# Late expert blocks as two halves of 64 rows, each with an expert of its own, multiplied in two halves of TensorE's columns

## The chip, the core and the metric

One core of one Trainium2 chip runs the whole program in one launch. The metric is the device time of that launch in microseconds (us). TensorE multiplies: its array of 128 x 128 holds a stationary operand (up to 128 columns, loaded by an LDWEIGHTS that the profile shows as PEld) and streams a moving operand through it; the result lands in PSUM, one partition for each stationary column. VectorE (DVE), ScalarE (ACT) and GpSimd (POOL) do the elementwise work, SyncE (SP) issues most DMAs, GpSimd the indirect ones. All data are float32.

## The reference

Two layers on x of 4 batches x 512 tokens x 512 channels. Layer 0 is a gate (a two-sided decayed sum over the 512 positions), a Mamba2 state-space block, a second gate and a feed-forward part with experts. Layer 1 is a gate, an attention block (16 heads in 4 groups), a gate and a dense feed-forward part. The change lies in layer 0's experts, which compute this, with E = 8 experts and the two best of them for each token:

```python
logits = x @ gate_w.T + gate_b
top_vals, top_idx = jax.lax.top_k(logits, 2)
routing = softmax(top_vals)
for e in range(8):
    h = x @ w1[e].T + b1[e]                  # w1[e]: 1024 x 512
    x_glu, x_lin = h[:, 0::2], h[:, 1::2]
    y = x_glu * sigmoid(1.702 * x_glu) * (x_lin + 1.0)
    ye = y @ w2[e].T + b2[e]                 # w2[e]: 512 x 512
    out = out + ye * sum(routing * (top_idx == e))[:, None]
```

Here x is 2048 tokens x 512 channels, the output of the second gate. The reference multiplies every token by every expert. Only 2 x 2048 = 4096 pairs of a token and an expert have a weight that is not zero.

## The kernel before, in words

**Blocks.** The kernel computes only those 4096 pairs. It sorts them by expert into blocks of 128 rows, and a block has one expert. How many blocks an expert needs is known only when the routing has been computed on the chip, so the program holds NBLK = 39 blocks, as many as any routing can need, of which ALWAYS = 37 are always run and the last two stand behind a branch on the number of blocks in use (L1557).

**Early and late.** The batches come out of the Mamba2 stage one after the other. Full blocks of the first three batches can be formed before the fourth is routed: at least NEARLY = 17 of them, the *early* blocks, which the program interleaves with the end of the Mamba2 stage of the fourth batch (`rounds()`, L1297). The other 22 are *late* blocks and run after it. The late blocks are again ordered so that those with rows of batch 0 come first (FIRST = 15 of them), because the layer's next step starts with batch 0.

**Finding the rows.** `route()` (up to L620) computes for each pair its block and its place in it. It builds tables with VectorE (`ov`, `os`) and multiplies them on TensorE (`ptok`, L604), two times four matmuls with VectorE's second pair of tables between them, so that `toks` holds in column s and row v the id of the pair in place s of block v. `logits()` (L498) is in front of it: for each quarter of the batch the products `pl`, and transposes `pht` of the gated rows, which go to a table `rows_h` in HBM. `order_blocks(lo, hi)` (L648) then decides which blocks of the table become the program's blocks lo to hi-1. It is called for the early blocks (L1437) and for the late ones (L1537). VectorE finds which blocks are in use; TensorE sums them (`pidx<-use`, L663 and following); VectorE builds a selection `of` (L686); TensorE multiplies with it (`pidx<-of`, L689 and L690); VectorE turns the result into `idx_h` (which rows to fetch), `eb` (the expert of each block) and `idx_o` (where to scatter). All blocks that follow wait for this.

**A round.** `class Experts` runs the blocks as a pipeline, one `round()` (L865) for each block i. Every product is 4 matmuls of a 128 x 128 stationary piece with 512 moving columns:

- `fetch` (L771): GpSimd gathers the 128 rows of block i+3 from `rows_h` by an indirect DMA.
- `flip` (L783): TensorE transposes the rows of block i+1 (`pfl`, 4 transposes), ScalarE copies them into `hT`.
- `first_half`: `pg` (L812), then `pn` (L823), the two halves of w1 for block i, with biases, Tanh and products on VectorE and ScalarE between.
- `finish` (`pyt`): 4 transposes of block i-1's y; ScalarE copies them, halved, into `yT`.
- `down` (`po`, L845): the product with w2 for block i-2, a bias on VectorE, and GpSimd's scatter into `rows_o` (L851).

A block of the table that is not in use writes its rows to row 0 of `rows_o`, which nobody reads.

**Weights.** An expert's weights are two halves of w1 (`w<-in_w1x`, 1 MB each), w2 (1 MB) and broadcast biases b1 and b2 (512 and 256 KB). SyncE reads the expert of a block from `eb` and issues the loads under the condition that it differs from the one that the slot holds. Early blocks use slot 0. Late blocks use slot i % 2, so that a late block's weights are loaded while the block before it runs. `second_weights` (L857) loads w2 when the last `down` that reads the slot has been issued.

**What sets the order.** The program is written as one stream, and a scheduler orders the instructions of each engine from it by a priority that is, roughly, the place in the stream, and by when it expects the operands to be ready: an instruction that waits can be overtaken by a later one that is ready, when the program is built. On the chip each engine then runs its instructions in that fixed order. `with after(engine)` (L88) pins the instructions in it behind the one of that engine that was recorded last. `more()` (L1523) runs late rounds, and after each it lets `pump` issue pieces of layer 1's gates (VectorE's `num`, `den`, `eu` with ScalarE), 1 or 2 per round. During the last rounds, `load_results` (L1481) and `add_results` bring batch 0's rows back from `rows_o` and transpose them on TensorE (`pcb`, L1500) into x.

L1190 (`pyd`) and L1033 (`ppr`), which the prediction's steps use as rows, belong to the Mamba2 stage: L1033 has a stationary operand of 64 columns between matmuls of 128.

Of the kernel before, what the change touches and what calls it, by code (L numbers as in the profile page):

```python
# [36 lines left out]
NBLK = (B * T * TOPK + E * (P - 1)) // P  # L37
NROW = B * T * TOPK + 1

NEARLY = -(-((B - 1) * T * TOPK - E * (P - 1)) // P)  # L40

ALWAYS = NBLK - 2

FIRST = (T * TOPK + E * (P - 1)) // P
# [39 lines left out]
def block_kernel(ctx: ExitStack, tc: tile.TileContext, a: dict, out: bass.AP):  # L84
# [374 lines left out]
    res_id = [count(f"res{c}", [[TOPK * T, B], [P, NT]], 1, 1 + c * T) for c in range(2)]  # L459
# [6 lines left out]

    places = tmp.tile([P, NBLK], I32, tag="th", name="places")
    for lo, hi in ((0, FIRST), (FIRST, ALWAYS - NEARLY), (ALWAYS - NEARLY, NBLK - NEARLY)):
        half = (hi - lo + 1) // 2
        nc.gpsimd.iota(places[:, lo : lo + 2 * half], pattern=[[1, half], [half, 2]], base=lo,  # L470
                       channel_multiplier=0)
    place = rt.tile([P, NBLK - NEARLY], F32, name="place")
    nc.vector.tensor_copy(place, places[:, : NBLK - NEARLY])
# [171 lines left out]
    eb = rt.tile([1, NBLK + 1], I32, name="eb")  # L645
    in_use = eb[:, NBLK:]

    def order_blocks(lo, hi):  # L648

        n = hi - lo  # L650
        cv = rt.tile([P, 1], F32, tag="cv", name="cv")
        nc.vector.tensor_tensor(jk, sel, cnt[:, (N2 if lo else N2 - NT), :], ALU.mult)
        nc.vector.tensor_reduce(cv, jk, AX.X, ALU.add)
        use = rt.tile([P, 1], F32, tag="use", name="use")
        if lo == 0:
            nc.vector.scalar_tensor_tensor(use, v_lo, float(P), cv, ALU.add, ALU.is_le)
        else:
            nc.vector.tensor_tensor(use, v_lo, cv, ALU.is_lt)
            nc.vector.tensor_tensor(use, use, taken, ALU.subtract)
        pi = ps_tp("pidx")  # L660
        rank = rt.tile([P, 1], F32, tag="vrank", name="vrank")
        if lo == 0:
            nc.tensor.matmul(pi[:, P : P + 1], lhsT=tri_lt, rhs=use, start=True, stop=True)  # L663
            nc.vector.tensor_copy(rank, pi[:, P : P + 1])
        else:

            two = rt.tile([P, 2], F32, tag="two", name="two")
            nc.vector.tensor_tensor(jk, sel, cnt[:, NT, :], ALU.mult)
            nc.vector.tensor_reduce(rank, jk, AX.X, ALU.add)
            nc.vector.tensor_scalar(two[:, 0:1], v_lo, rank, use, ALU.is_lt, ALU.mult)  # L670
            nc.vector.tensor_tensor(two[:, 1:2], use, two[:, 0:1], ALU.subtract)
            nc.tensor.matmul(pi[:, P : P + 2], lhsT=tri_lt, rhs=two, start=True, stop=True)
            nc.tensor.matmul(pi[:, P + 2 : P + 3], lhsT=ones, rhs=two[:, 0:1], start=True, stop=True)
            nc.tensor.matmul(pi[0:1, P + 3 : P + 4], lhsT=ones[:, 0:1], rhs=use, start=True, stop=True)
            nc.vector.tensor_copy(in_use, pi[0:1, P + 3 : P + 4])

            nc.vector.tensor_scalar(
                rank, pi[:, P + 1 : P + 2], pi[:, P + 2 : P + 3], two[:, 1:2], ALU.add, ALU.mult
            )
            nc.vector.scalar_tensor_tensor(  # L680
                rank, pi[:, P : P + 1], two[:, 0:1], rank, ALU.mult, ALU.add
            )
        if lo == 0:
            nc.vector.scalar_tensor_tensor(taken, rank, float(n), use, ALU.is_lt, ALU.mult)
        of = tmp.tile([P, NBLK], F32, tag="th", name="of")
        nc.vector.tensor_scalar(  # L686
            of[:, :n], place if lo else lane[:, :n], rank, use, ALU.is_equal, ALU.mult
        )
        nc.tensor.matmul(pi[:, :n], lhsT=toks, rhs=of[:, :n], start=True, stop=True)  # L689
        nc.tensor.matmul(pi[0:1, 2 * P : 2 * P + n], lhsT=v_e, rhs=of[:, :n], start=True, stop=True)  # L690

        gf = tmp.tile([P, NBLK], F32, tag="th", name="gf")
        nc.vector.tensor_scalar(gf[:, :n], pi[:, :n], NROW - 2.0, None, ALU.add)
        nc.vector.tensor_copy(idx_h[:, lo:hi], gf[:, :n])
        low = tmp.tile([P, NBLK], I32, tag="th", name="low")
        nc.vector.tensor_scalar(
            low[:, :n], idx_h[:, lo:hi], T - 1, (B - 1) * T, ALU.bitwise_and, ALU.bitwise_xor
        )
        nc.vector.tensor_scalar(
            idx_h[:, lo:hi], idx_h[:, lo:hi], 1, (B - 1) * T,  # L700
            ALU.logical_shift_right, ALU.bitwise_and,
        )
        nc.vector.tensor_tensor(idx_h[:, lo:hi], idx_h[:, lo:hi], low[:, :n], ALU.bitwise_xor)
        ef = tmp.tile([1, NBLK], F32, tag="th", name="ef")
        nc.vector.tensor_scalar(ef[:, :n], pi[0:1, 2 * P : 2 * P + n], E - 1.0, None, ALU.add)
        nc.vector.tensor_copy(eb[:, lo:hi], ef[:, :n])
        nc.vector.tensor_copy(idx_o[:, lo:hi], pi[:, :n])

    class Experts:
# [13 lines left out]
        def open(self):  # L723
# [5 lines left out]
            self.load_w1(1, 0, 0)  # L729
            self.load_w2(0, 0)  # L730
# [9 lines left out]
        def slot(self, i):  # L740
            return 0 if i < NEARLY else i % 2

        def load_w1(self, h, s, e, **kw):

            nc.sync.dma_start(
                out=self.w1[s][h].rearrange("p k i -> p (k i)"),
                in_=a["w1x"][e, :, h * NC * I : (h + 1) * NC * I], **kw
            )
            if h == 1:
                nc.sync.dma_start(  # L750
                    out=self.b1[s].rearrange("p a i -> p (a i)"),
                    in_=a["b1x"][e].partition_broadcast(P), **kw
                )

        def load_w2(self, s, e, **kw):
            nc.sync.dma_start(out=self.w2[s].rearrange("p k m -> p (k m)"), in_=a["w2x"][e], **kw)
            nc.sync.dma_start(out=self.b2[s], in_=a["b2x"][e].partition_broadcast(P), **kw)

        def know(self, n):
# [4 lines left out]
            if n > NEARLY:  # L764
                self.weights(self.i if n == NBLK else NEARLY)
# [22 lines left out]
        def weights(self, i, early=False):  # L788
# [3 lines left out]
            s = self.slot(i)  # L792
            e = nc.sync.value_load(eb[0:1, i : i + 1], min_val=0, max_val=E - 1)
            kw = {"cond": e != self.held[s]} if s in self.held else {}
            self.held[s] = e
            self.reg[i] = s, bass.ds(e, 1), kw
            self.load_w1(0, *self.reg[i][:2], **kw)
# [4 lines left out]
        def more_weights(self, i):  # L802
            if i in self.reg:
                s, e, kw = self.reg[i]
                self.load_w1(1, s, e, **kw)

        def first_half(self, i):

            s, hT, sm = self.reg[i][0], self.hT.pop(i), self.sm
            pg = ps_mm("pg")  # L810
            for k in range(NC):
                nc.tensor.matmul(  # L812
                    pg, lhsT=hT[:, k, :], rhs=self.w1[s][0][:, k, :],
# [1208 lines left out]
```

## Time and profile before

| what | value |
|---|---|
| median of 3 runs | 2245.44 us (2244.33 to 2245.93) |
| the profiled execution's own time | 2248.54 us |
| its span (first to last instruction) | 2246.8 us |
| mean granted TensorE clock | 0.978 of full speed |
| TensorE busy by stage, us of the stretch | 0 to 664: 589.79 of 664.00 |
| | 664 to 790: 119.65 of 126.00 |
| | 790 to 890: 96.05 of 100.00 |
| | 890 to 1123: 231.62 of 233.00 |
| | 1123 to 2246.8: 1094.71 of 1123.80 |
| VectorE busy, 890 to 1123 | 146.44 |
| DMA engines busy, 890 to 1123 | 0.82 (296 GB/s) |

How to read it. The span is counted from the first recorded instruction; the time of the execution is 1.7 us longer because it has what lies around the instructions. The early blocks start within the stretch 664 to 790, when the fourth batch is still in the Mamba2 stage and being routed, and the late blocks fill the stretch 890 to 1123. A line of the trace such as `L812 MATMUL pg<-w,hT 128*128 128x512 f32 x8` tells the kernel's line, the tile written and the tiles read, the stationary operand (rows * columns), the moving one, and how many records follow each other; a float32 matmul leaves two records. In a timeline the first two columns are the start and how long the group took, and what stands in brackets is the time for which the engine was idle before it, and who released it.

### The profile page before, as it was taken

The numbers are of one execution on the slowest core, as the hardware profiler recorded it, in microseconds if no ns is written. First come the engines' busy times: TensorE is split into PE (matmuls) and PEld (weight loads), VectorE is DVE, ScalarE is ACT, GpSimd is POOL, SyncE is SP. The second block draws the span as 40 slices with busy tenths as digits, with TensorE's granted clock in tenths as the row PEclk, the third lists the DMA queues.
The fourth block names the chain that finished last, engine by engine and source line by source line (L and its number), as shares of the span: only waits on it lengthen the run. The fifth ranks groups of instructions, "written<-read, shape, count | busy, mean of one in ns | idle before, by whom it ended". The sixth has DMA issues, their size and how long they took to land. (4 is left out here: it accounts for less than half of the span.)

```text
span 2246.8 us, 23747 instructions
## 1 busy us (share of the span) xinstructions
PE 2131.8 (95%) x7528; PEld 1228.1 (55%) x7528; DVE 1526.6 (68%) x3039; ACT 969.5 (43%) x1899; POOL 451.5 (20%) x620
## 2 busy tenths in 40 slices
PE   2879999999999999999988999999999999999998
PEld 1445565565665444444444455555555555568887
DVE  8698989989753556666477766677767765555332
ACT  4476676765842233433154333333334332333221
POOL 4023232331222111222112111112212122100000
PEclk9889999999999999999989999999999999999999
DMA  7542252341433357988576655555645564531100
GB/s 257 176 146 71 95 164 74 128 141 67 135 124 126 146 201 268 367 299 310 206 241 200 188 183 150 159 164 176 183 143 173 142 195 141 178 130 38 38 20 20
DMA packets 112452, 357.38 MB, mean 159 GB/s; under 512 B 14592, under 2 KB 23168, under 8 KB 102912
## 3 DMA queue, kind: packets, MB, share of 16 engines
q1 hardware_dynamic: 78656, 224.43, 28.8%
q0 software_dynamic: 31360, 127.16, 18.9%
q10 hardware_dynamic: 2304, 4.20, 0.5%
q8 instruction: 62, 1.02, 0.2%
q14 instruction: 70, 0.57, 0.1%
HBM read 337.91 MB, written 108.00 MB: 198 GB/s over the span
## 5 line engine op out<-in xcount | busy, mean ns | idle before, releaser
L1677 POOL DMA_DIRECT2D turned<-turned x248 | 136.0, 555 | 621.4 <-DVE turned L1669 387.0
L128 ACT ACTIVATE pr<-psc,nmax 128x128 f32<-128x128 f32 (+3 forms) x256 | 134.7, 527 | 286.9 <-DVE nmax L1658 286.6
L1631 PE MATMUL pq<-h,wq 128*128 128x512 f32 x512 | 237.4, 599 | 1.6 <-DVE h L404 1.0
L1736 PE MATMUL pd<-cx,wd 128*128 128x512 f32 x512 | 222.4, 592 | 0.0
L1052 PE MATMUL pc<-h,wxb 128*128 128x512 f32 x320 | 149.1, 622 | 44.1 <-DVE h L1311 39.0
L1744 DVE TENSOR_TENSOR xr<-xr,pd 128x512 f32<-128x512 f32 x64 | 44.0, 687 | 196.9 <-PE pd L1736 196.9
L1653 PE MATMUL psc<-kT,qT 128*128 128x128 f32 (+3 forms) x512 | 159.9, 442 | 15.1 <-ACT pr L128 14.1
L1736 PEld LDWEIGHTS pd<-cx,wd 128*128 128x128 f32 x512 | 96.1, 190 | 114.8 <-issue 110.2
L1631 PEld LDWEIGHTS pq<-h,wq 128*128 128x128 f32 x512 | 94.8, 193 | 102.2 <-issue 91.2
L1721 PE MATMUL pctx<-pT,v 128*128 128x512 f32 (+3 forms) x512 | 148.4, 433 | 0.0
L1721 PEld LDWEIGHTS pctx<-pT,v 128*128 128x128 f32 x512 | 96.7, 190 | 76.2 <-issue 50.5
L845 PE MATMUL po<-w,yT 128*128 128x512 f32 x296 | 134.2, 593 | 0.9 <-DMA w<-in_w2x 0.6
L812 PE MATMUL pg<-w,hT 128*128 128x512 f32 x296 | 133.9, 593 | 0.0
L823 PE MATMUL pn<-w,hT 128*128 128x512 f32 x296 | 133.4, 593 | 0.5 <-DMA w<-in_w1x 0.5
L1052 PEld LDWEIGHTS pc<-h,wxb 128*128 128x128 f32 x320 | 62.2, 200 | 116.5 <-issue 74.5
L1653 PEld LDWEIGHTS psc<-kT,qT 128*128 128x128 f32 x512 | 85.0, 191 | 73.4 <-issue 28.7
L1658 DVE TENSOR_REDUCE nmax<-psc 128x1 f32<-128x128 f32 (+3 forms) x256 | 122.3, 481 | 2.1
L1669 DVE STREAM_TRANSPOSE turned<-pr 128x128 f32<-128x128 f32 x248 | 117.2, 494 | 1.2
L1123 PE MATMUL pz<-wzt,h 128*128 128x512 f32 x256 | 115.8, 601 | 0.3 <-ACT st L1224 0.3
L1271 PE MATMUL po<-wot,yT 128*128 128x512 f32 x256 | 115.2, 604 | 0.0
L1665 DVE TENSOR_SCALAR pr<-pr,rsum 128x128 f32<-128x128 f32 (+3 forms) x256 | 95.8, 376 | 2.2
L1656 DVE TENSOR_TENSOR psc<-psc,mask 128x128 f32<-128x128 f32 x256 | 71.0, 285 | 37.3 <-PE psc L1653 36.8
(344 smaller groups left out, 4179.1 us busy)
## 6 DMA issues: line engine op xcount, KB each, us to landing
w<-in_w1x SPq DMA_DIRECT2D x76, 1024.0 KB
turned<-turned POOLq DMA_DIRECT2D x248, 208.0 KB, 3.8
pT<-turned POOLq DMA_DIRECT2D x62, 832.0 KB, 7.3
w<-in_w2x SPq DMA_DIRECT2D x38, 1024.0 KB
wb<-in_b1x SPq DMA_DIRECT2D x38, 512.0 KB
lm<-cs SPq DMA_DIRECT2D x32, 512.0 KB
kt<-in_fT SPq DMA_DIRECT2D x62, 256.0 KB
ek<-ek SPq DMA_DIRECT2D x62, 256.0 KB
```

The costliest lines, as they stand in the source:

```text
L128: nc.scalar.activation(*args, **kw)
L812: nc.tensor.matmul(pg, lhsT=hT[:, k, :], rhs=self.w1[s][0][:, k, :], start=(k == 0), stop=(k == NC - 1))
L823: nc.tensor.matmul(pn, lhsT=hT[:, k, :], rhs=self.w1[s][1][:, k, :], start=(k == 0), stop=(k == NC - 1))
L845: nc.tensor.matmul(po, lhsT=yT[:, j, :], rhs=self.w2[s][:, j, :], start=(j == 0), stop=(j == NI - 1))
L1052: nc.tensor.matmul(pc, lhsT=wxb[:, k, m * P : (m + 1) * P], rhs=h[:, k, :], start=(k == 0), stop=(k == NC - 1),)
L1631: nc.tensor.matmul(pq, lhsT=u.wq[:, k, i * KVC : (i + 1) * KVC], rhs=u.h[:, k, :], start=(k == 0), stop=(k == NC - 1),)
L1653: nc.tensor.matmul(psc[:, :n], lhsT=qT[:, qi * P : n], rhs=u.kT[:, :n], start=True, stop=True)
L1658: nc.vector.tensor_reduce(nmax, psc[:, :n], AX.X, ALU.max, negate=True)
L1669: nc.vector.transpose(blocks[:, :, 3 * qi : 4 * qi + 1, :].rearrange("p c k j -> p k c j"), pr)
L1677: nc.gpsimd.dma_start(out=d[:, :, r].rearrange("c i s -> i c s"), in_=blocks[r * SQ : (r + 1) * SQ].rearrange("i c k j -> i c (k j)"),)
L1721: nc.tensor.matmul(pctx[:, kj * P :].rearrange("p (q r j) -> p q r j", r=QUAD, j=SQ), lhsT=u.v[:, kj, :], rhs=pT[:, :, 4 * kj : 10 + kj : ...
L1736: nc.tensor.matmul(po, lhsT=dense_w[u.g][:, i, m * P : (m + 1) * P], rhs=u.ctxT[i], start=(i == 0), stop=(i == HPG - 1),)
```

## The change

Late blocks no longer have one expert. A late block is two halves of HALF = 64 rows, rows 0 to 63 (left) and 64 to 127 (right), and each half has its own expert. The pairs of an expert that were not taken by early blocks are cut into halves of 64; the first half of the halves, in order, go to the left side and the others to the right side, within each of the groups (with rows of batch 0, without, behind the branch). Early blocks stay whole.

- **Counts.** NBLK 39 becomes 36, ALWAYS 37 becomes 34, FIRST 15 becomes 12; NLATE = 19 late blocks have 38 entries for experts in `eb`. The branch is taken when more than 2 x (34 - 17) = 34 halves are in use.
- **Weights.** Slot 0 belongs to the left half (and to the early blocks), slot 1 to the right half; each late round can change either. The biases of both halves go into one tile, each into its own 64 partitions. `know()` loads the first right expert unconditionally.
- **Products.** `product()` issues, for each of the 4 pieces, one matmul for an early block and two for a late one: `hT[:, k, 0:64]` with the left expert's weights into partitions 0 to 63, and `hT[:, k, 64:128]` with the right expert's into 64 to 127. Each of these is pinned with `after(nc.tensor)`, in early blocks too.
- **Order in the round.** For late blocks `flip(i + 1)` is recorded right after `finish` (pinned), no longer before `first_half`. w2 is reloaded when the next `down` is that of the block.
- **order_blocks** becomes `order_early()` and `order_late()`. The latter ranks 64-row halves in two groups, with small tiles taken from the rotating pool `tmp`, two products per side and table column for `pidx<-of`, and is recorded where the late call stood.
- **Gates.** After a late round `pump` takes the steps 5i // 3 - 5(i - 1) // 3, so 5 in 3 rounds; before it was 3 in 2. `rows_o` has one more row, since the right side's unused rows go to row 1.

The core of the diff (the tile names, `of`, `low` and so on are those of the listing above):

```diff
+HALF = P // 2
-NROW = B * T * TOPK + 1
+NROW = B * T * TOPK + 2
-NBLK = (B * T * TOPK + E * (P - 1)) // P
+NBLK = -(-((B * T * TOPK + E * (HALF - 1)) // HALF) // 2)
-FIRST = (T * TOPK + E * (P - 1)) // P
+FIRST = -(-((T * TOPK + E * (HALF - 1)) // HALF) // 2)
+NLATE = NBLK - NEARLY
+SIDES = (slice(0, HALF), slice(HALF, P))
...
+    def order_early():
+        n = NEARLY
+        cells = tmp.tile([P, 3], F32, tag="th", name="cells")
+        cv, use, rank = (cells[:, i : i + 1] for i in range(3))
+        nc.vector.tensor_tensor(jk, sel, cnt[:, N2 - NT, :], ALU.mult)
...
+    def order_late():
+        n = NLATE
+        cells = tmp.tile([P, 8, 2], F32, tag="th", name="cells")
+        use, front, back, rank, both, low = (cells[:, i, :] for i in range(6))
...
+        nc.tensor.matmul(pi[:, P : P + 2], lhsT=tri_lt, rhs=both, start=True, stop=True)
+        nc.tensor.matmul(pi[:, P + 2 : P + 3], lhsT=ones, rhs=both[:, 0:1], start=True, stop=True)
...
+        ahead_of = tmp.tile([P, 3], F32, tag="th", name="ahead_of")
+        nc.vector.tensor_copy(ahead_of, pi[:, P : P + 3])
...
+        of = tmp.tile([P, 2, 2, NLATE], F32, tag="th", name="of")
+        for h in range(2):
...
+            nc.vector.tensor_scalar(of[:, h], place, r, use[:, h : h + 1], ALU.is_equal, ALU.mult)
+        for side, rows_ in enumerate(SIDES):
+            for h in range(2):
+                nc.tensor.matmul(
+                    pi[rows_, :n], lhsT=toks[:, h * HALF : (h + 1) * HALF], rhs=of[:, h, side, :],
+                    start=(h == 0), stop=(h == 1),
+                )
...
     class Experts:
...
-        def slot(self, i):
-            return 0 if i < NEARLY else i % 2
+        def sides(self, i):
+            return (slice(0, P),) if i < NEARLY else SIDES
+        def load_b1(self, e, rows_, **kw):
+            nc.sync.dma_start(
+                out=self.b1[int(rows_ in SIDES)][rows_].rearrange("p a i -> p (a i)"),
+                in_=a["b1x"][e].partition_broadcast(rows_.stop - rows_.start), **kw
+            )
...
         def know(self, n):
...
+            if n == NBLK:
+                self.weights(self.i)
+            elif n > NEARLY:
+                self.first = [self.expert(NEARLY, s) for s in range(2)]
+                left, right_ = (bass.ds(e, 1) for e in self.first)
+                self.load_w1(0, 1, right_)
+                self.load_w1(1, 1, right_, SIDES[1])
+                self.load_w2(1, right_, SIDES[1])
+                self.load_b1(left, SIDES[0])
+                self.load_b2(left, SIDES[0])
...
+        def product(self, i, out_, xT, w, k, n):
+            for s, rows_ in enumerate(self.sides(i)):
+                with after(nc.tensor):
+                    nc.tensor.matmul(
+                        out_[rows_], lhsT=xT[:, k, rows_], rhs=w(s)[:, k, :],
+                        start=(k == 0), stop=(k == n - 1),
+                    )
...
             for k in range(NC):
-                nc.tensor.matmul(
-                    pg, lhsT=hT[:, k, :], rhs=self.w1[s][0][:, k, :],
-                    start=(k == 0), stop=(k == NC - 1)
-                )
+                self.product(i, pg, hT, lambda s: self.w1[s][0], k, NC)
...
         def second_weights(self, down):
-            for i in list(self.w2_due):
-                s, e, kw = self.reg[i]
-                if all(self.slot(j) != s for j in range(max(down + 1, 0), i)):
-                    self.load_w2(s, e, **kw)
-                    self.w2_due.remove(i)
+            while self.w2_due and self.w2_due[0] <= max(down + 1, 0):
+                for s, e, rows_, kw in self.reg[self.w2_due.pop(0)]:
+                    self.load_w2(s, e, rows_, **kw)
...
         def round(self):
...
                 self.weights(i)
-                if i >= NEARLY:
-                    self.weights(i + 1)
                 self.flip(i)
-                if self.ahead:
+                if self.ahead and i < NEARLY:
                     with after(nc.tensor):
                         self.flip(i + 1)
                 half = self.first_half(i)
                 next(half)
-                if i + 1 < NEARLY:
-                    self.weights(i + 1, True)
+                self.weights(i + 1, True)
             if i - 1 in self.y:
                 with after(nc.tensor):
                     self.yT[i - 1] = self.finish(self.y.pop(i - 1))
+            if self.ahead and i < self.known:
+                with after(nc.tensor):
+                    self.flip(i + 1)
             if i - 2 in self.yT:
                 self.down(i - 2)
...
-            lo = 1 + int(AT[b]) + c * T + t * P
+            lo = 2 + int(AT[b]) + c * T + t * P
...
-                        pump(1 + moe.i % 2)
+                        pump(5 * moe.i // 3 - 5 * (moe.i - 1) // 3)
...
-        order_blocks(NEARLY, NBLK)
+        order_late()
         moe.know(ALWAYS)
-        more(NBLK - 8)
+        more(ALWAYS - 6)
...
-        with tc.If(used > ALWAYS - NEARLY):
+        with tc.If(used > 2 * (ALWAYS - NEARLY)):
```

## The prediction, made before the changed kernel had run

> **What bounds the kernel now.** Times are us, positions count from the span's start. I read the page first: what is busy, and what the chain that ended last consists of.
>
> ```profile
> PE 2131.8 (95%) x7528; PEld 1228.1 (55%) x7528; DVE 1526.6 (68%) x3039; ACT 969.5 (43%) x1899; POOL 451.5 (20%) x620
> ...
> PE 40%; DVE 7%; ACT 1%; DMA 0%; issue 0%; DVEq 0%; ACTq 0%
> ```
>
> TensorE bounds it. Then the expert stage, by windows: its late blocks run from 889.75 to 1122.7 with TensorE busy 231.86 of 232.95, so there a round costs what TensorE's instructions cost. The timeline of TensorE gives one late round:
>
> ```profile
> 1004.97 3.60 PE L812 MATMUL pg<-w,hT 128*128 128x512 f32 x8
> 1008.40 0.60 PE L836 MATMUL pyt<-ident,u 128*128 128x128 f32 x4
> 1008.84 3.60 PE L823 MATMUL pn<-w,hT 128*128 128x512 f32 x8
> 1012.28 0.60 PE L783 MATMUL pfl<-ident,hb 128*128 128x128 f32 x4
> 1012.71 3.60 PE L845 MATMUL po<-w,yT 128*128 128x512 f32 x8
> 1016.15 0.59 PE L812 MATMUL pg<-w,hT 128*128 128x512 f32 x1
> ```
>
> A round is 1016.15 - 1004.97 = 11.18. A product is 8 records (4 matmuls, each recorded twice), one every 0.43; a transpose comes every 0.11. The 0.59 of one record is its length with the way through the array, and the next starts before it ends.
>
> **The late rounds.** Counting the reference's routing on its inputs, the experts get 445, 1766, 393, 17, 483, 772, 163 and 57 rows: 37 blocks of 128 (the trace has 296 = 37 x 8 records of pg), or 68 halves of 64. Less the 17 early blocks that leaves 20 rounds now and 34 halves = 17 rounds after. The branch is taken above 34, so it stays closed.
>
> Every late product becomes twice as many matmuls, of 64 stationary columns each. No row shows two halves of the array at work together. A 64-column matmul is no shorter: L1033 streams its 128 columns in 0.107 like the 128-column L1190. So serial halves cost 24 x 0.43 = 10.3 more a round; fully overlapped, nothing. I take the overlap: the two halves share no column, weight or output partition, and L812 shows TensorE using each part as it frees (the load for the next matmul starts 0.002 after the running one starts). A matmul's two records need the same columns, so half B runs one record behind half A: 0.43 a round for filling.
>
> Rounds also switch the array between halves and whole. That price is in the trace:
>
> ```profile
> 356.24 0.39 PE L1190 MATMUL pyd<-skip,xc 128*128 128x128 f32 x2
> 356.71 0.43 PE L1033 MATMUL ppr<-tri_le,dtv 128*64 128x128 f32 x2
> 357.07 0.49 PE L1190 MATMUL pyd<-skip,xc 128*128 128x128 f32 x2
> ```
>
> From the last whole record (356.35) to the first 64-column one lie 0.36 instead of 0.11, and its load adds 0.05: 0.30. Coming back, the record at 357.07 starts 0.09 late and is 0.10 long over: 0.20. The stall at 513.7 has the same nanoseconds. The built program puts pyt and pfl side by side, so a round switches once each way: 0.50. A round becomes 11.18 + 0.43 + 0.50 = 12.11; 17 x 12.11 - 20 x 11.18 = **-17.7**. The four pcb transposes of the last rounds stand alone between pn and pg, one more switch each: **+2.0**.
>
> The row says that loads hide under matmuls on the same rows. The Trainium skill, "TensorE: Matmul & The Clock Gate", section "Part 3: Packing small matmuls — row/col tiling", says a weight load overlaps a running matmul only when the row group differs, which speaks against this change, as both halves use all rows; it also reports three column tiles at 2.38 times one, which no row here shows. By that rule all 48 loads a round stand open, an estimate of 48 x 0.053 x 17 = 43 us more; the trace's own loads contradict it for a whole array.
>
> **Weights.** Now late blocks alternate between two slots; after, each side has one, and a slot can be reloaded only between the product that read it last and the same product of the next round, 8.3 us (pn, pg, transposes, switches). Early blocks have one slot already: at block 16's change po sat 0.60 and pn 0.53 for weights, in all 1.5 lost; the two changes before cost nothing. The late order has 11 changes after block 17's preload, with both sides at block 21, while DMA is at 0.99 share from 912 to 981. Bounds 0 and 11 x 1.5 = 16; I take **+6**, the middle of hidden and paid.
>
> **Order on TensorE: the part the words of the change don't tell.** product() pins every matmul behind the instruction recorded before it, in early blocks too. Today the scheduler slips expert matmuls into waits:
>
> ```profile
> 766.70 1.05 PE L604 MATMUL ptok<-os,ov 128*128 128x128 f32 x8
> 767.59 3.60 PE L812 MATMUL pg<-w,hT 128*128 128x512 f32 x8
> 771.02 1.02 PE L845 MATMUL po<-w,yT 128*128 128x512 f32 x2
> 772.46 1.16 PE L604 MATMUL ptok<-os,ov 128*128 128x128 f32 x8 [0.42 <-DVE ov L597]
> ...
> 781.05 1.98 PE L812 MATMUL pg<-w,hT 128*128 128x512 f32 x4
> 785.04 0.40 PE L689 MATMUL pidx<-of,toks 128*128 128x22 f32 x2 [2.01 <-DVE of L686]
> ```
>
> In the built program of the changed kernel this filling is gone. Place by place:
> - ptok: all 16 records stand together. pg and two records of po (10 x 0.43) no longer lie before the second eight, and VectorE's ov is ready when it was: **+4.3**.
> - order_late: pidx<-of follows the prefix products directly. VectorE's list from pn's last start T to the second of: 0.63, u 0.69, ahead_of 0.15, u 0.67, then gate work put between (num 1.27, den 1.2 twice, den 1.27, den 0.68, eu 0.69, num 0.67) and some ten small operations at 0.1 to 0.3, less 0.07 overlap each: about T + 10.3. TensorE is through at T + 1.0: 9.3 idle instead of 2.0, **+7.3**, and 0.5 for its 64-column products.
> - last gate's logits: pl and pht of three parts stand together. From pht's end (709.22) ScalarE's hr copy and tanh and VectorE's h_last end at 711.26: 2.1 idle, twice, where pg, po and pn lie now. With the two pg records ahead of pot (0.86): **+5.1**.
> - order_early: its tile comes from a pool of two, so its first sum moves behind ov and os; the gather goes from 663.8 to about 664.4: **+0.6**.
>
> Together +17.8. TensorE is dense there now (idle 0.4 and 2.0 apart), so these waits lengthen the span; VectorE uses them for gate work, which is not on the path. VectorE busy 146.4 of 233 in the late stage stays off it: 136 of about 206.
>
> Clock: after an idle of 4.87 at 162.15 the clock was granted at half from 163.06 to 169.88, 2.9 of it after work resumed; an idle of 2.01 at 783 brought nothing. For two long waits and the pair of 2.1: 1.5 + 2.2 + 0.8 = **+4.5**, bounds 0 and three times 3.4 = 10.
>
> At nothing: ten conditional DMAs a round on SyncE instead of five. A skipped one takes 0.45, an issued one 0.7, so 4.5 to 7 of a round of 12; what that delays is in the weights' bounds (the right side's w2 queues behind a bias load that waits for VectorE's o). Half the bias bytes, the pace of the gates (one step fewer), one row more in rows_o and the side table lie beside TensorE's work.
>
> **Sum.** -17.7 + 2.0 + 6 + 17.8 + 4.5 = **+12.6**. The profiled execution took 2248.5 (span 2246.8), 3.1 above the median of the runs, 2245.4; it would become 2261.1, and the median **2258.0**.
>
> **Rivals.**
> - *The waits are covered* (faster). TensorE passes a waiting pidx or ptok, or VectorE comes to of before its gate work. Then 17.8 + 4.5 shrink; below 9.7 in all (17.7 - 2.0 - 6) the gain wins. At nothing: -9.7, 2235.7. Against: L689 idles 2.01 today with four ready pg records behind it, and each engine's trace follows the built order. 0.14.
> - *Loads not hidden.* Matmul B's load waits until A's second record has started: two loads of 0.053 open per matmul pair, 12 x 0.107 = 1.3 a round, +22: 2280. 0.14.
> - *Halves don't overlap*, so the change doesn't do what it says: +10.3 x 17 = 175, 2433. For: no row shows overlap of products. 0.10.
> - *Weights far later*: 30 instead of 6, 2282. For: DMA share 0.99. 0.04.
>
> The forecast has 0.58, with a range of its own from 2244 to 2272 (clock 0 and weights 0 below; clock 10 and weights 16 above, nearly). 0.2%, 4.5 us, is about what a measurement can tell from no change; 0.12 of the forecast's chance lies in it. Faster 0.14, same 0.12, slower 0.46 + 0.14 + 0.10 + 0.04 = 0.74. The range 2236 to 2290 leaves out the serial case and the edges of two rivals.
>
> **What would show it.** Late pg starts 12.1 apart (11.2: no fill or switch; 13.4: open loads; 22: serial). 34 x 8 = 272 records of 64-column pg, two to each 0.43. pidx<-of idle near 9, ptok near 4.7, two waits of 2 at pl, and half clock after them. If these waits are small, the sign is wrong; if weight waits at pg, pn, po exceed 16 together, the size is.

## The result, and the profile after

The changed kernel takes 2274.24 us (median of 4 runs, 2264.14 to 2276.40) against 2245.68 (median of 4, 2244.33 to 2248.88): slower, by a ratio of 1.0116 (95% interval 1.0084 to 1.0148). The profiled execution took 2273.76, its span is 2272.0.

The page of the changed kernel, busy times and the chain that ended last:

```profile
PE 2113.6 (93%) x7850; PEld 1194.8 (53%) x7850; DVE 1521.1 (67%) x3038; ACT 962.1 (42%) x1890; POOL 443.3 (20%) x617
...
PE 40%; DVE 7%; DMA 1%; ACT 1%; issue 0%; SPq 0%; DVEq 0%; ACTq 0%
```

TensorE is busy 18.2 less (2131.8 - 2113.6) in a span that is 25.2 longer: 43.4 more idle. DMA has 1% of the chain now instead of 0%, and SyncE's queue (SPq) appears on it.

The timeline of TensorE in a late round without waits:

```profile
1028.64 3.60 PE L875 MATMUL pg<-w,hT 128*64 128x512 f32 x16
1032.18 0.66 PE L903 MATMUL pyt<-ident,u 128*128 128x128 f32 x4
1032.67 0.60 PE L844 MATMUL pfl<-ident,hb 128*128 128x128 f32 x4
1033.20 3.65 PE L875 MATMUL po<-w,yT 128*64 128x512 f32 x16
1036.69 3.60 PE L875 MATMUL pn<-w,hT 128*64 128x512 f32 x16
1040.12 3.60 PE L875 MATMUL pg<-w,hT 128*64 128x512 f32 x16
```

16 records of half the columns take the 3.60 that 8 records of all columns took: the halves overlap fully. A round is 1040.12 - 1028.64 = 11.48, only 0.30 more than before, though it has 48 matmul records.

The timeline of TensorE where the routing is computed, with the idle time before an instruction in brackets:

```profile
702.65 1.06 PE L507 MATMUL pl<-gw,h_last 128*128 128x8 f32 x8 [1.93 <-DVE h_last L408]
...
706.22 1.84 PE L507 MATMUL pl<-gw,h_last 128*128 128x8 f32 x8 [2.02 <-DVE h_last L408]
...
708.81 5.05 PE L875 MATMUL pg<-w,hT 128*128 128x512 f32 x8
...
772.16 2.07 PE L608 MATMUL ptok<-os,ov 128*128 128x128 f32 x8 [4.71 <-DVE ov L601]
...
795.41 1.03 PE L732 MATMUL pidx<-of,toks 128*64 128x19 f32 x8 [8.27 <-DVE of L729]
```

These are the waits of the prediction: 2 twice at pl, near 4.7 at ptok, near 9 at pidx<-of. After the second pl, ptok and pidx<-of the work runs at half clock for a while: pg at 708.81 takes 5.05 instead of 3.60.

The timeline of TensorE at four changes of an expert:

```profile
954.58 1.94 PE L875 MATMUL pg<-w,hT 128*64 128x512 f32 x2 [3.01 <-DMA w<-in_w1x]
...
987.48 1.07 PE L875 MATMUL po<-w,yT 128*64 128x512 f32 x2
989.95 3.22 PE L875 MATMUL po<-w,yT 128*64 128x512 f32 x13 [1.41 <-DMA w<-in_w2x]
...
1000.40 0.66 PE L903 MATMUL pyt<-ident,u 128*128 128x128 f32 x4
...
1015.39 5.39 PE L875 MATMUL pg<-w,hT 128*64 128x512 f32 x16 [6.25 <-DMA w<-in_w1x]
...
1055.14 5.34 PE L875 MATMUL pg<-w,hT 128*64 128x512 f32 x14 [2.53 <-DMA w<-in_w1x]
```

At 954.58, 1015.39 and 1055.14 pg waits for the first half of w1, and runs at half clock after. At 989.95 po waits for w2. Here two records of one half were done before the wait, so the halves are out of step after it: the three products up to 1000.40 take 12.92 - 1.41 = 11.51 without the wait, where po, pn and pg of the round above take 10.46, all at full clock. A wait of one side thus costs more than its idle time. All waits for weights from block 17's pg on sum to 18.66. In the 13 us up to the end of the longest, 6.25, the DMA engines have a share of 0.98 to 1.03 (the columns are those of the windows below; the last two are DMA share and GB/s):

```profile
1002.00:1006.00 4.00, 4.00 (x21) 1.40 (x19) 0.69 (x1) 0.17 (x1) 0.73 (x1) 1.00 0.98 329
1006.00:1010.00 4.00, 3.14 (x14) 1.34 (x10) 1.39 (x2) 0.63 (x1) 0.99 (x1) 1.00 1.03 363
1010.00:1015.40 5.40, 0.01 (x2) 0.04 (x2) 5.26 (x6) 1.08 (x2) 0.00 (x0) 0.69 0.99 378
```

**The two traces by stage.** "Early" runs from the first pg to block 17's first pg, "late" from there to the first pk of layer 1.

| | up to the first pg | early | late | after it | span |
|---|---|---|---|---|---|
| before | 671.70 | 218.05 | 237.48 | 1119.59 | 2246.82 |
| after | 664.04 | 238.38 | 245.87 | 1123.75 | 2272.04 |
| difference | -7.7 | +20.3 | +8.4 | +4.2 | +25.2 |

The windows of the kernel before, early and late (the columns: stretch, its length, busy time of TensorE, of its loads, of VectorE, ScalarE and GpSimd, granted clock, DMA share, GB/s), and then those of the kernel after:

```profile
671.70:889.75 218.05, 210.89 (x656) 103.86 (x655) 111.53 (x203) 59.77 (x93) 42.23 (x51) 1.00 0.52 180
889.75:1127.23 237.48, 232.50 (x671) 110.67 (x669) 149.16 (x190) 80.12 (x113) 48.83 (x50) 1.00 0.81 292
```

```profile
664.04:902.42 238.38, 217.51 (x662) 108.82 (x661) 121.36 (x225) 66.91 (x100) 39.65 (x51) 0.95 0.50 172
902.42:1148.29 245.87, 217.60 (x985) 79.02 (x985) 132.97 (x168) 65.96 (x97) 38.12 (x40) 0.97 0.74 250
```

Early, idle time goes from 218.05 - 210.89 = 7.2 to 20.9 (+13.7), and nearly the same work is busy 6.6 longer, at a clock of 0.95. Late, busy time falls by 14.9 and idle time rises from 5.0 to 28.3. The -7.7 ahead of the first pg is not put down to the change: in the fourteen traces here the first pg starts between 659.07 and 678.72, and the half-clock stretches ahead of it differ from execution to execution. So stages are compared below, and medians.

### The profile page after: what moved, and what is told of

The parts are those of the page before. It is cut to its first block, busy times and chain, and to the rows that moved or that the text cites. A ratio compares the mean times of both kernels' runs of the same rounds, so it can differ in the third digit from the quotient of the medians.

```text
span 2272.0 us, 24801 instructions
## 1 busy us (share of the span) xinstructions
PE 2113.6 (93%) x7850; PEld 1194.8 (53%) x7850; DVE 1521.1 (67%) x3038; ACT 962.1 (42%) x1890; POOL 443.3 (20%) x617
## 5 line engine op out<-in xcount | busy, mean ns | idle before, releaser
L875 PE MATMUL pg<-w,hT 128*64 128x512 f32 (+1 forms) x408 | 136.8, 634 | 16.3 <-DMA w<-in_w1x 16.3
L875 PE MATMUL pn<-w,hT 128*64 128x512 f32 (+1 forms) x408 | 124.1, 593 | 1.7 <-DMA w<-in_w1x 1.7
L875 PE MATMUL po<-w,yT 128*64 128x512 f32 (+1 forms) x408 | 124.4, 597 | 1.4 <-DMA w<-in_w2x 1.4
```

What stands on the lines that cost most here:

```text
L875: nc.tensor.matmul(out_[rows_], lhsT=xT[:, k, rows_], rhs=w(s)[:, k, :], start=(k == 0), stop=(k == n - 1),)
```

## The experiments

My theory after the result: the pin on early products costs the early +20.3; the waits for weights cost more than the late rounds gain; the halves themselves gain. The rivals stand in the expectations. The result of all, with stages from the trace of each:

| | median us | ratio to before (interval) | early | late | waits for weights, late |
|---|---|---|---|---|---|
| before | 2245.68 | | 218.05 | 237.48 | 0 |
| after | 2274.24 | 1.0116 (1.0084-1.0148) | 238.38 | 245.87 | 18.66 |
| e1_free_early | 2270.35 | 1.0130 (1.0096-1.0165) | 228.32 | 253.01 | 20.61 |
| e2_before_pin_early | 2262.64 | 1.0102 (1.0072-1.0132) | 237.55 | 237.69 | 0 |
| e3_no_reload | 2244.68 | 1.0018 (0.9998-1.0037) | 239.97 | 218.81 | 0.31 |
| e4_side_by_side | 2300.49 (one run) | | 237.88 | 274.43 | 7.02 |
| e5_preload_later | 2269.07 | 1.0120 (1.0056-1.0185) | 223.50 | 249.11 | 20.49 |
| e6_tail_split | 2264.36 | 1.0090 (1.0059-1.0121) | 217.60 | 250.59 | 19.29 |
| e7_keys_gpsimd | 2254.29 | 1.0048 (1.0028-1.0069) | 216.51 | 243.89 | 16.96 |
| e8_gates_first | 2290.61 | 1.0217 (1.0162-1.0271) | 257.78 | 238.90 | 17.57 |
| e9_quarter_bytes | 2249.54 (one run) | | 239.82 | 219.16 | 3.60 |
| e10_before_keys | 2240.53 | 0.9998 (0.9982-1.0013) | 216.65 | 237.49 | 0 |
| e11_no_pin | 2254.18 | 1.0062 (1.0035-1.0089) | 217.29 | 238.60 | 15.75 |
| e12_keys_tail | 2246.17 | 1.0023 (1.0005-1.0042) | 218.10 | 236.42 | 14.13 |

The kernel before, run beside the experiments, had medians of 2242.1 to 2242.6 with single runs from 2234.6 to 2250.3.

### e1_free_early: the pin kept for late products only

```diff
-                with after(nc.tensor):
+                with after(*(() if i < NEARLY else (nc.tensor,))):
                     nc.tensor.matmul(out_[rows_], lhsT=xT[:, k, rows_], ...
```

> The changed kernel with the pin of the products kept for late blocks only; early products may again be slipped into waits, as before. Theory (the pin in early blocks is the largest loss): pidx<-of waits below 1 instead of 8.27, ptok about 0.4 instead of 4.71, the two waits of 1.93 and 2.02 at pl gone, and with them the half clock after them (3.42 + 3.41 + 5.12 lost): 16 to 26 less, 2248 to 2258. Rival (the longer list of order_late on VectorE is what delays the late rounds, pinned or not): pidx<-of still waits 6 or more, 2264 to 2268. Rival (the halves and their weights are the loss): within 3 of the changed kernel, 2274.

2270.35, hardly less than 2274 and outside the theory's range. Yet the waits at pl are gone and pidx<-of waits 0.35 instead of 8.27; ptok still waits 3.00, not 0.4 as the theory had it. The timeline of TensorE in this run shows where the gain went:

```profile
769.51 2.07 PE L608 MATMUL ptok<-os,ov 128*128 128x128 f32 x8 [3.00 <-DVE ov L601]
...
791.77 0.29 PE L732 MATMUL pidx<-of,toks 128*64 128x19 f32 x2 [0.35 <-DVE cells L728]
...
802.57 5.45 PE L875 MATMUL pg<-w,hT 128*128 128x512 f32 x8 [5.66 <-DMA w<-in_w1x]
```

Early blocks still wait, 5.66, at a place where the kernel after had no wait, put down to w1. SyncE's own timeline there:

```profile
796.36 0.90 SPq L784 DMA_DIRECT2D w<-in_w1x  x2
797.44 0.57 SPq L792 DMA_DIRECT2D wb<-in_b1x  x1
798.20 1.76 SPq L798 DMA_DIRECT2D w<-in_w2x  x1
800.21 0.51 SPq L803 DMA_DIRECT2D wb<-in_b2x  x1
800.91 0.47 SPq L792 DMA_DIRECT2D wb<-in_b1x  x1
801.56 0.47 SPq L803 DMA_DIRECT2D wb<-in_b2x  x1
802.46 0.09 SPq L784 DMA_DIRECT2D w<-in_w1x  x1
```

The load that pg waits for is the last line: it is skipped (0.09), but stands behind the seven unconditional loads of know(). With the pin, pidx<-of had hidden this. The early stage is 10.1 shorter than after, not 20; the late stage of this execution, 7.1 longer (2.2 more idle, nearly all of it waits for weights, and 4.9 more busy at a clock of 0.95 instead of 0.97), took most of it back.

### e2_before_pin_early: the kernel before, with the pin on early products

```diff
             for k in range(NC):
-                nc.tensor.matmul(pg, lhsT=hT[:, k, :], ...
+                with after(*((nc.tensor,) if i < NEARLY else ())):
+                    nc.tensor.matmul(pg, lhsT=hT[:, k, :], ...
```

(the same for pn and po)

> The kernel before with one thing of the change alone: every product of an early block pinned behind the TensorE instruction recorded before it. Theory (the pin costs this by itself): ptok waits 4.7, pl 2.0 twice, pidx<-of 3.7 (its 2.0 and the 4 pg records that no longer lie before it), half clock after the longer ones: 10 to 20 more than before, 2255 to 2266. Rival (the pin matters only together with order_late's list): 0 to 4 more, 2246 to 2250.

2262.64, about 20 more than the kernel before beside it. Its timeline has the waits of the kernel after:

```profile
707.39 1.87 PE L503 MATMUL pl<-gw,h_last 128*128 128x8 f32 x8 [1.93 <-DVE h_last L404]
...
712.23 1.84 PE L503 MATMUL pl<-gw,h_last 128*128 128x8 f32 x8 [2.02 <-DVE h_last L404]
...
778.06 2.08 PE L604 MATMUL ptok<-os,ov 128*128 128x128 f32 x8 [4.71 <-DVE ov L597]
...
796.86 0.62 PE L689 MATMUL pidx<-of,toks 128*128 128x22 f32 x2 [3.92 <-DVE of L686]
```

1.93, 2.02 and 4.71 to the digit; pidx<-of 3.92 with the short list, where order_late's longer one makes it 8.27. Early is +19.5 (of after's +20.3), late +0.2. The pin by itself costs nearly the whole early loss in this trace. By idle time alone it is 10.2 of the 13.7; the longer list accounts for the rest (8.27 - 3.92 = 4.35 at pidx<-of).

### e3_no_reload and e9_quarter_bytes: what the weights cost

e3 issues no reload behind block 17; e9 issues every one, with a quarter of the bytes of w1 and w2.

```diff
             self.reg[i] = []
+            if i > NEARLY:
+                return
```

> The changed kernel without the reloads of weights after block 17: all later late blocks multiply with the first two experts' weights, so this part of the output is another one; the work of TensorE is the same. Theory (the waits for weights cost what the trace shows): 18.2 of waits at pg, pn and po after block 17's pg go, and up to 8.5 lost to half clock at 954, 1012 and 1056 with them: 2247 to 2256. Rival (the weights' waits stand in for other waits that would come anyway, VectorE or the gathers): less than 8 gained, 2266 to 2274.

```diff
+            n_ = 1 if rows_ in SIDES and kw else NC
-                out=self.w1[s][h].rearrange("p k i -> p (k i)"),
+                out=self.w1[s][h].rearrange("p k i -> p (k i)")[:, : n_ * I],
```

(the source likewise, and w2)

> The changed kernel whose conditional reloads of w1 and w2 in late blocks bring only the first quarter of each megabyte (the rest keeps the weights of the expert before, so this part of the output is another one); every instruction and every place in SyncE's queue stays. Theory (the late waits for weights are bytes: the rate of the DMA engines and the gates' loads ahead): the waits at pg, pn and po from block 17 on fall from 18.66 to below 6, and the half clock after them goes. Rival (they are SyncE's order: loads issued late behind waits for other loads and behind the reads of the expert table): 12 or more remain.

e3: 2244.68, a little below the range expected. e9: 2249.54 in one run. Both have a late stage of 219, 27 less than after, and the waits are down to 0.31 and 3.60. The traced execution of e3 took 2260.30, the longest of its ten; its late stage alone is used. The window of that stage:

```profile
918.69:1137.51 218.82, 208.55 (x986) 76.76 (x985) 132.32 (x168) 65.40 (x98) 39.25 (x45) 0.98 0.37 120
```

DMA share 0.37 instead of 0.74; TensorE idles 10.3 instead of 28.3 (18.0 less), and the same work is busy 9.0 less, at a clock of 0.98 instead of 0.97. So the weights cost 27: 18 of waits, and 9 of longer work. The clock's records account for at most half of the 9 (half clock takes 8.5 of the late stage after and 4.2 in e3); the rest fits halves that are out of step, as at 989.95. As e9 keeps every instruction and place of SyncE's queue, it is the bytes that are late, not the order of their issue. Without the reloads the late stage is 18.7 shorter than before: that is what the halves are worth in e3's trace, with its 4.2 of half clock. In e9 the late stage is at full clock (1.00), and 219.16 less its 3.60 of waits for weights is 21.9 shorter than before.

### e4_side_by_side: four matmuls of the left half, then four of the right

```diff
+            ks = (k,) if i < NEARLY else range(n) if k == 0 else ()
             for s, rows_ in enumerate(self.sides(i)):
+                for k in ks:
                     with after(nc.tensor):
```

> The changed kernel with the four matmuls of the left half issued first and the four of the right half after them, instead of taking turns; same work. Theory (two matmuls overlap only when they are neighbours in TensorE's one queue and use different columns): nothing overlaps but the one pair in the middle, a late product takes nearly 16 x 0.43 instead of 8 x 0.43, a round about 21, in all some 150 to 175 more: 2425 to 2450. Rival (each half of the columns takes its work on its own): no change, 2274.

2300.49: neither theory. A round is 1052.94 - 1039.48 = 13.46, 2.0 more than after and far from serial. Its timeline, from po on:

```profile
1039.48 4.13 PE L877 MATMUL po<-w,yT 128*64 128x512 f32 x13
1043.02 0.64 PE L877 MATMUL pn<-w,hT 128*64 128x512 f32 x1
1043.45 0.59 PE L877 MATMUL po<-w,yT 128*64 128x512 f32 x1
...
1052.94 0.64 PE L877 MATMUL po<-w,yT 128*64 128x512 f32 x1
```

Left records of pn run between right records of po, which stand ahead of them in the queue: here TensorE starts work for the free half about four records before its turn (in the trace the first right record starts 1.77 behind the first left one, beside the fifth). The halves need not be neighbours; what is lost is about four records, 4 x 0.43 = 1.7, in each run between whole-array transposes, in which one half works alone. Waits for weights are 7.02 only; a longer round leaves the loads more time, which no run isolates.

### e5_preload_later: know() one round later

```diff
         order_late()
+        more(moe.i + 1)
         moe.know(ALWAYS)
```

> The first experiment's kernel (pin on late products only), and know() with its seven unconditional loads called one round after order_late instead of before that round. Theory (the 5.66 at pg, put down to w1, are SyncE's queue: the next early block's own load, which is skipped, stands behind these seven and the reads of the expert table): the 5.66 and the half clock after it go, 7 to 9 less than the first experiment: 2261 to 2264. Rival (pg waits for data that really has to come): the wait stays within 2 of 5.66, 2268 or more.

2269.07 (two runs, 2263.72 and 2274.43). The 5.66 fell to 1.70 and early by 4.8, most of what the theory has; the medians cannot tell this apart, and in this execution the first pg came late, at 676.25.

### e6_tail_split: the sum of results ahead of po (on e5)

```diff
+            before()
             if i - 2 in self.yT:
                 self.down(i - 2)
+            behind()
             self.second_weights(i - 2)
```

(before() computes rr on ScalarE and VectorE; behind() does the pcb transposes and the sum into x)

> As the kernel with know() one round later, and in the last four rounds the sum of results (rr) is recorded ahead of po and its transposes (pcb) right behind po, instead of both behind the round. Theory (the pinned pn leaves pcb to wait for VectorE's u, u and rr): the four waits at pcb, 2.30, 2.28, 1.54 and 1.55 in the first experiment, fall below 2.5 together, and nothing else takes their place: 4 to 6 less than with know() later alone, 2256 to 2259. Rival (pk waits for the last results of the scatter anyway): the waits move to pk, within 2.

2264.36. The waits at pcb fell from 7.66 to 4.25, not below 2.5. The last two, where no pn is left, are gone; the first two, where pn now stands behind pcb, are 2.08 and 2.17:

```profile
1091.94 0.66 PE L1566 MATMUL pcb<-ident,rr 128*128 128x128 f32 x4 [2.08 <-DVE rr L1558]
1092.52 5.35 PE L875 MATMUL pn<-w,hT 128*64 128x512 f32 x16
```

pk waits 3.85 instead of 2.41, and pyt 1.61 in the last of these rounds. The theory held for two of four places; by waits the whole gain is under 1. The medians can't tell, with two runs of e5; the traced execution, 2249.22, is the shortest of e6's seven.

### e7_keys_gpsimd and e10_before_keys: the gates' loads from GpSimd

```diff
-            nc.sync.dma_start(out=kt[i], in_=a["fT"][cc * P : (cc + 1) * P, b, :])
+            key_queue[0].dma_start(out=kt[i], in_=a["fT"][cc * P : (cc + 1) * P, b, :])
...
+        key_queue[0] = nc.gpsimd
         moe.ahead = True
```

(ek and ekv likewise; e7 on e5, e10 on the kernel before)

> As the kernel with know() one round later, and the loads for layer 1's gates (kt, ek, ekv) in the late stage issued by GpSimd instead of SyncE. Theory (the weights wait because these loads, 1.5 MB in a row, stand ahead of them in one queue): the waits for weights from block 17 on, 19.2 in the first experiment, fall below 10 and the half clock after them mostly goes: 2248 to 2256. Rival (it is the rate of the DMA engines, whichever queue): the waits stay at 15 or more, 2260 to 2266. A third way (GpSimd's gathers are held up behind these loads): waits at pfl appear, slower than 2266.

> The kernel before with nothing of the change, and the loads for layer 1's gates in the late stage issued by GpSimd. Theory (these loads are in the way only where one slot per side must be reloaded within a round): no change to the kernel before, within 4. Rival (GpSimd's queue is the better place for them in any case): 5 or more faster than before.

e7: 2254.29, faster than e5 by 0.7% (1.0048 against 1.0120), but not for the reason given. The waits for weights sum to 16.96, as the rival said; only the longest fell (5.07 and 5.46 in e5, none above 2.66 here), and with them what half clock takes late, 10.2 to 7.7. After the move, the change of expert that is at 1015.39 above, where six of these loads (1.5 MB) had been issued from 1001.31 to 1004.43, waits less:

```profile
988.67 3.65 PE L877 MATMUL pn<-w,hT 128*64 128x512 f32 x14 [1.17 <-DMA w<-in_w1x]
...
994.43 5.35 PE L877 MATMUL pg<-w,hT 128*64 128x512 f32 x16 [2.12 <-DMA w<-in_w1x]
```

Early is 7.0 less than in e5's trace, and ptok waits 0.42 again instead of 3.00, as VectorE's ov comes sooner. But e6, with ptok at 2.99, has an early stage of 217.60 in its trace, so most of the 7.0 is where half clock fell. That the scheduler orders VectorE's gate work otherwise once these loads leave SyncE's queue is argued from the order alone; no run isolates it. In the kernel before the same move does nothing (e10: 0.9998).

### e8_gates_first: the gates' work ahead of the late rounds (on e5)

```diff
-                        pump(5 * moe.i // 3 - 5 * (moe.i - 1) // 3)
+                        pump(3 if moe.i <= NEARLY else 1)
```

> As the kernel with know() one round later, and the pump after each round takes 3 steps up to block 17 and 1 step later, instead of 5 in 3 rounds throughout; so most of the gates' loads and VectorE's work are moved ahead of the rounds in which weights change. Theory (the gates' loads get in the way of the weights): waits for weights from block 17 on below 10, 2250 to 2257. Rival (the weights' own 3 MB for each side are the load): 15 or more, 2260 to 2266. Rival (VectorE cannot do 3 steps a round): waits of pyt or po for u and o between 800 and 890, slower than 2262.

2290.61: VectorE cannot do 3 steps a round. TensorE's timeline:

```profile
818.95 1.09 PE L903 MATMUL pyt<-ident,u 128*128 128x128 f32 x4 [5.57 <-DVE u L897]
...
881.67 1.09 PE L903 MATMUL pyt<-ident,u 128*128 128x128 f32 x4 [7.66 <-DVE u L897]
```

pyt's waits sum to 27.4. Late, the waits for weights stay at 17.57 with 18 of the gates' loads in this stage instead of 29: the second rival holds too, by the waits. The gates' loads are not most of what the weights wait for: fewer of them take 2.9 off the 20.49 of e5, while e9, with all 29 and a quarter of the weights' bytes, takes 15.1 off the 18.66 of after.

### e11_no_pin and e12_keys_tail: what is left

e11 takes the pin from all products; e12 has the pin on late products and the split tail; both with know() later and the gates' loads on GpSimd.

> The changed kernel with no product pinned at all, know() one round later and the gates' loads on GpSimd. Theory (the pin on late products does nothing for the overlap, as the halves overlap even 8 records apart, and only keeps pcb from being covered): a late round stays at 11.5, the waits at pcb fall from 7.7 by 1 to 4; 2250 to 2254. Rival (without the pin the halves are issued apart): rounds above 11.8, 2258 or more.

> All that helped, together: pin on late products only, know() one round later, the gates' loads on GpSimd, the sum of results ahead of po in the last four rounds. Theory (the losses are separate terms): 2 to 4 less than with the gates' loads on GpSimd alone (2254), 2249 to 2253, so still above the kernel before, by the waits for weights that remain (17) less the gain of the rounds. Rival (they hide one another): 2254 or more.

e11: 2254.18, pcb waits 5.94 (1.7 less than in e7), a round still 11.48 (1005.52 to 1017.00), and the time is e7's: the pin on late products does nothing for the overlap. e12: 2246.17, 3 below the range of its theory, at 1.0023 (1.0005 to 1.0042) of the kernel before: what remains of the loss is about 0.2%. Early is 218.10, that of before. Late is 236.42, 1.1 less than before, with 14.13 of waits for weights still in it. Why it is 8 less than e7 in the medians is not shown: the split tail alone saves 0.4 of waits there (pcb, pk and pyt together 9.7 instead of 10.1), while in these traces the waits for weights are 2.8 less and half clock takes 2.1 of the late stage instead of 7.7. No version tried beats the kernel before.

## Why the prediction was right in direction and short in size

The forecast was +12.6; the medians moved by 28.6. 2274.24 lies just above the forecast's own range (2244 to 2272) and inside the whole one (2236 to 2290).

- **Late rounds** (-17.7): the overlap was right, the round too dear. Forecast 12.11, measured 11.48, so 17 x 11.48 - 20 x 11.18 = -28.4. The 0.43 for filling is not paid: in the trace the right half starts 0.007 behind the left. The switch costs 0.30 a round, not 0.50: 0.15 between pg and pyt, 0.15 between pfl and po. The price had been read at L1190 and L1033, where the array changes every two records; and the profile puts 0.28 of idle time of TensorE's loads ahead of L1033 down to ScalarE's `ex`, so that row held a wait for data and was no clean price of a switch.
- **Loads.** The prediction weighed the Trainium skill, "TensorE: Matmul & The Clock Gate", section "Part 3: Packing small matmuls — row/col tiling", by which a weight load overlaps a running matmul only when the row group differs, against the trace. The measurement decides for the trace: 16 records with their 16 loads take 3.60, so the loads lie beside matmuls on the same rows. As 8 whole-array records take 3.60 too, two column tiles of 64 do twice the work of one in that time.
- **pcb** (+2.0): 7.69 of waits instead of 2.63, so +5.1, and in some traces half clock behind them (3.4 in e3, none in after and e9). The switches had been counted, but not that pcb is left to wait while VectorE does u, u and rr; e6 and e11 change the order there and take 3.4 and 1.7 off. At full clock -28.4 + 5.1 and an estimate of about 1 for the switches (4 x 0.30) make -22.3, near the -21.9 of e9; with 3.4 of half clock -18.9, near the -18.7 of e3.
- **Weights** (+6, bounds 0 and 16): measured 27 against e3 (30 against e9 without its own waits). This is the term that was mis-sized. The price of a change was taken from block 16, where 1.5 was lost at a slot's change at a DMA share of 0.87 (870 to 889.75); the late changes come in a row and on both sides, with a DMA share of 0.98 to 1.03 from 1002 to 1015 while pg waits. The prediction's sign for a wrong size, waits of more than 16 together, came true at 18.66. The 9 of longer work behind these waits, half clock and halves out of step, was not in the sum at all.
- **Order on TensorE** (+17.8): mechanism and places held, and the sizes nearly. ptok has +4.29 (forecast 4.3); pl, pht and pot together 5.05 (5.1); pidx<-of +6.26 (7.3), and 0.8 for its products, at half clock (0.5). In all 13.7 more is idle early, as pyt waits 1.5 less. e2 shows that the pin is the main cause; order_late's list adds 4.4 to one of the waits.
- **Clock** (+4.5): 6.6 more of busy time early, behind just these waits.
- **Sum.** Early +20.3 (forecast 22.3 with the clock) and late +8.4 (forecast -9.7) make 28.7. That this is so near to the 28.6 of the medians is partly luck, as both come from one trace each; the -7.7 and +4.2 outside them lie within what the stages there vary by from trace to trace (up to the first pg 659.07 to 678.72, after pk 1119.05 to 1124.47). The sign came from the early stage, which was right. The size was off by the late one, where, reckoned by e3, two misses of opposite sign, -10.7 at the rounds and +21 at the weights, left 10 more, and pcb 8 more. So it is luck, too, that the time came as near to the forecast as it did: the better round hid half of the miss at the weights.

Of the rivals, "waits covered" fell (the order built is the order run, all waits came); "loads not hidden" and "halves don't overlap" fell with the 3.60; and "weights far later" (30, given 0.04) was the one that came nearly true, on top of a better round.

## What to carry to other kernels

A pin that keeps two instructions together also forbids everything else that the scheduler slipped into waits: list what stood in each wait of the old trace, and pin only where the order is needed (here nowhere: without any pin, e11 keeps the round of 11.48). When a slot's double buffer is given up, work out bytes per round and not only the window: two sides of 3 MB in a round of 11.5 would be some 550 GB/s, an estimate against the 329 to 378 GB/s that were moved while pg waited; and a wait for them can be paid again by half clock and by halves out of step behind it. Where a gain goes missing after a repair (e1), look at the queue of the engine that issues: a load that is skipped still held TensorE (5.66) until the seven ahead of it had been issued.

## What the runs showed of the hardware that was not expected

- TensorE starts matmuls ahead of others in its own queue, by about four records, when the columns that they need are free (e4). Two halves of the columns take the time of one whole product when they alternate (3.60 for 16 records), and still overlap, less well, four by four (13.46 a round instead of 11.48).
- Half clock comes in steps: by the clock's records most stretches last 3.4, 6.8 or 10.2, half of which is lost where TensorE works. It follows waits, but not by their length alone: the wait of 2.53 was followed by a stretch of 3.4, the 2.27 at pcb by none in the kernel after and the 2.28 there by one of 3.4 in e1, and the 1.63 at 915.75 by none.
- Ahead of the first pg, which the experiments leave alone, these stretches differ from execution to execution, and the first pg starts anywhere from 659.07 to 678.72; single runs of the kernel before spread from 2234.6 to 2250.3.
